# Layer 0 of a graph network: wider search chunks for the neighbour lists, biases on TensorE, row copies on ScalarE

## The chip, the core and the metric

The kernel runs on one core of one Trainium2 chip. The metric is the device time of one execution in microseconds; a difference is read from the medians of runs on the same chip. The engines are written as in the profile: PE (TensorE), PEld (its weight loads), DVE (VectorE), ACT (ScalarE), POOL (GpSimd), SP (SyncE, which here only issues transfers). L417 is line 417 of the kernel before.

## What is computed

A graph of n = 3327 nodes with 256 features each passes through four attention layers. The adjacency is a 0/1 matrix, symmetric, with ones on the diagonal and about 32 other neighbours a row. Layer 0 is the one that the change touches:

```python
g_src = nodes @ W_src_w.T + W_src_b
g_tgt = nodes @ W_tgt_w.T + W_tgt_b
g = leaky_relu(g_src[:, None, :] + g_tgt[None, :, :], 0.2)
score = where(adj != 0, einsum('ijc,c->ij', g, a_w), -inf)
x = layernorm(x + softmax(score, axis=1) @ g_tgt)
```

Layers 1 to 3 are attention layers whose scores split into a row and a column part; they are computed densely, on PE with DVE, and none of their code changes.

## The kernel before

**Layer 0 by lists.** Nodes are cut in 26 tiles of 128 rows and these in three sets of 5, 9 and 12 tiles (`SETS`). For each row the kernel finds the column numbers of its neighbours, and then fetches, for each of the up to 56 places of a list, one row of a table in HBM for each of 128 nodes (`gather`, L544, an indirect transfer that POOL issues). Within a set the rows are ranked by their number of neighbours, so that each later tile has fewer places (`LEVELS`).

**Projections** (`targets`, `sources`, L347 to L379). For each tile two products on PE (`project`, L342, contraction in two halves of 128) give the target row (256 features and one more column, the target's own part of the score) or the source row. DVE adds the target bias, L358, and takes the source with its bias and a turned sign, L374. ScalarE copies the one extra column, L359, and issues the writes of the row to the table `table_d` and to `own_d`, which holds for each node its source, its input x and its target row. The x part of `own_d` is copied from HBM to HBM by POOL's queue at the start, for all three sets (L327). The columns that PE needs are loaded by SP (L337, four buffers).

**The search** (`neighbours(s)`, L391 to L496). A tile's adjacency rows come in two halves of 1664 columns, loaded by SP (L122, called at L411; two buffers). L417 turns a half into 16-bit numbers: 0 where there is no edge, n minus the column where there is one; it sums them too. The diagonal is taken out (L426, L430). Then MAX8 (L436), an instruction that gives the eight largest of a row, is run on chunks of 64 columns, 52 a tile. The first three of each chunk go to a list `few` (L441), the best eight of the rest are added (L445): 164 numbers. From these, seven rounds of MAX8 and MATCH_REPLACE8 (L448, L450) draw 56. The sum of all numbers minus the sum of the 56 is stored in `lost` (L458): if it isn't zero for any row, the program repeats everything densely at its end (L1609). The numbers become column indices (L460), the count becomes a sort key, which a product on PE spreads over partitions (L481), and L490 with L494 make the ranks. POOL writes the lists to HBM in ranked order (`write_list`, L503) and reads them back (`read_lists`, L511).

**Scores and sums.** For each eight places (a part): `score` on DVE (L563, L569), and at the end of a tile `combine`: exponentials and scaling on ScalarE (L639, L650), adding up on PE (L653). `lay_out` on ScalarE (L559, L560) prepares a tile. `put_back` writes the sums (L689).

**Order of the work.** In this stage the order on PE, DVE, ACT and POOL is that of the program text. At first `neighbours(0)` runs in turn with the 26 `targets`, one of its 33 steps after each (L802). Then the lists of set 0 are written and read, and a loop over 126 parts (L862) issues at each part: a share of the steps of the next set's search (`owed`), work that is due at that part, the gathers of the part four ahead, and the scores. The lists of set 1 are written from part 17 on, those of set 2 from part 59. Eleven buffers hold gathered parts. SP isn't in this list: a planner of the compiler chooses the order on SP's queue, by readiness and place in the text; the load of the weight of layer 1 (L749), for example, belongs to a late part.[...] The dense layers follow when the sums are written.

Of the kernel before, what the change touches and what calls it, by code (L numbers as in the profile page):

```python
# [8 lines left out]
F32 = mybir.dt.float32  # L9
# [5 lines left out]
ALU = mybir.AluOpType  # L15
AX = mybir.AxisListType
# [3 lines left out]
P = 128  # L20
# [5 lines left out]


KMAX = 56
CHUNK = 64
FIRST = 3  # L30


SETS = (5, 9, 12)
# [6 lines left out]
FAR = 1e6  # L40

ROW = 260
# [4 lines left out]
def gat_stack(  # L47
# [29 lines left out]
    nc = tc.nc  # L77
    n, dim = x.shape
# [20 lines left out]

    h = [nodes.tile([P, dim], F32, name=f"h{it}") for it in range(nt)]  # L100
    at_d = dram.tile([nt * P, n], BF16, name="at_d")
    table_d = dram.tile([nt * P, ROW], F32, name="table_d")

    EARLY = sum(SETS[:-1])
    w1 = const.tile([P, kc, dim + 2], F32, name="w1")
# [10 lines left out]
    def copy_rows(engine, dst, src):  # L116

        rows = dst.shape[0]
        whole = rows // 16 * 16
        for lo, hi in ((0, whole), (whole, rows)):  # L120
            if lo < hi:
                engine.dma_start(dst[lo:hi], src[lo:hi])  # L122
# [139 lines left out]

    def sparse0(lost):
        GROUP, TURNS, LEAD = 8, 11, 4
        starts = [sum(SETS[:s]) for s in range(len(SETS))]
        with ExitStack() as s0:
# [11 lines left out]
                )  # L280
            )

            w_tgt = const0.tile([P, kc, dim + 1], F32, name="w_tgt0")
            nc.sync.dma_start(w_tgt[:, :, :dim], w_tgt_t.rearrange("(c p) f -> p c f", p=P))
            a_row = load_row(const0, a_w, "a_row")
            bt_row = load_row(const0, b_tgt, "bt_row")
            w_src = const0.tile([P, kc, dim], F32, name="w_src0")
            nc.scalar.dma_start(w_src, w_src_t.rearrange("(c p) f -> p c f", p=P))
            bs_row = load_row(const0, b_src, "bs_row")
            for c in range(kc):  # L290
                t = io0.tile([P, dim], F32, tag="minus", name="dots0")
                nc.vector.tensor_mul(t, w_tgt[:, c, :dim], a_row)
# [9 lines left out]
            for lo, hi in halves:  # L302
                hi = -(-hi // P) * P
                rev_i = io0.tile([P, nt * P // 2], I32, tag="adj_i", name="rev_i")
                nc.gpsimd.iota(
                    rev_i[:, : hi - lo], pattern=[[-1, hi - lo]], base=n - lo,
                    channel_multiplier=0,
                )
                nc.vector.tensor_copy(rev[:, lo:hi], rev_i[:, : hi - lo])
# [14 lines left out]
            for s, size in enumerate(SETS):  # L324
                lo, hi = starts[s] * P, min(n, (starts[s] + size) * P)
                own_d.append(dram.tile([size * P, OWN], F32, name=f"own{s}_d"))
                copy_rows(nc.gpsimd, own_d[s][: hi - lo, dim : 2 * dim], x[lo:hi, :])  # L327

            def own_rows(it):
                s = max(s for s in range(len(SETS)) if starts[s] <= it)  # L330
# [6 lines left out]
                nc.sync.dma_start(xt[:, :, :pn], x_t_p[:, :, it * P : it * P + pn])  # L337
                return xt, pn

            def project(p, xt, pn, weight):  # L340
                for k in range(kc):
                    nc.tensor.matmul(  # L342
                        p[:pn, : weight.shape[2]], xt[:, k, :pn], weight[:, k, :],
                        start=(k == 0), stop=(k == kc - 1),
                    )

            def targets(it):  # L347

                xt, pn = columns_of(it)
                row = io0.tile([P, ROW], F32, tag="row", name="row", bufs=3)  # L350
                nc.vector.memset(row[:, dim:], 0.0)
                if pn < P:
                    nc.vector.memset(row[:, :dim], 0.0)
                    nc.vector.memset(row[:, dim : dim + 1], -FAR)
                pt = ps0.tile([P, BANK], F32, tag="acc", name="pt")
                project(pt, xt, pn, w_tgt)
                yield
                nc.vector.tensor_add(row[:pn, :dim], pt[:pn, :dim], bt_row[:pn])  # L358
                nc.scalar.copy(row[:pn, dim : dim + 1], pt[:pn, dim : dim + 1])  # L359
                nc.scalar.dma_start(table_d[it * P : (it + 1) * P, :], row)  # L360
                nc.scalar.dma_start(own_rows(it)[:, 2 * dim :], row)
                yield

            def sources(it):

                xt, pn = columns_of(it)
                pss = ps0.tile([P, BANK], F32, tag="ps", name="pss", bufs=1)
                project(pss, xt, pn, w_src)
                yield
                minus = io0.tile([P, dim], F32, tag="minus", name="minus")  # L370
                if pn < P:
                    nc.vector.memset(minus, 0.0)
                    nc.scalar.dma_start(own_rows(it)[pn:, dim : 2 * dim], minus[pn:])
                nc.vector.scalar_tensor_tensor(  # L374
                    minus[:pn], pss[:pn, :dim], -1.0, bs_row[:pn],
                    op0=ALU.mult, op1=ALU.subtract,
                )
                nc.scalar.dma_start(own_rows(it)[:, :dim], minus)
                yield  # L379

# [6 lines left out]
            ]  # L387

            len_c = nt * P // CHUNK

            def neighbours(s):  # L391

# [7 lines left out]
                for t in range(size):  # L400
# [7 lines left out]
                    for b, (lo, hi) in enumerate(halves):  # L408
                        w, padded = hi - lo, -(-(hi - lo) // P) * P
                        adj_i = io0.tile([P, nt * P // 2], I32, tag="adj_i", name="adj_i")  # L410
                        copy_rows(nc.sync, adj_i[:pn, :w], adj[it * P : it * P + pn, lo:hi])  # L411
                        v = io0.tile([P, wider], U16, tag="num", name="num")
                        if pn < P:
                            nc.vector.memset(v, 0.0)
                        elif w < padded:
                            nc.vector.memset(v[:, w:padded], 0.0)
                        nc.vector.scalar_tensor_tensor(  # L417
                            v[:pn, :w], adj_i[:pn, :w], 0.0, rev[:pn, lo:hi],
                            op0=ALU.not_equal, op1=ALU.mult, accum_out=sums[:pn, b : b + 1],
                        )  # L420
                        if lo <= it * P < hi:

                            at0 = it * P - lo
                            own_v = v[:, at0 : at0 + P]
                            junk = io0.tile([P, P], F32, tag="junk", name="junk")
                            nc.vector.scalar_tensor_tensor(  # L426
                                junk, own_v, -1.0, ident, op0=ALU.mult, op1=ALU.mult,
                                accum_out=sums[:, 2:3],
                            )
                            nc.vector.tensor_mul(own_v, own_v, off_diag)  # L430
                        chunks = padded // CHUNK
                        for c in range(chunks):
                            if c == chunks // 2:
                                next(of_rows if b else before, None)
                                yield
                            nc.vector.max(  # L436
                                cand[:, lo // CHUNK + c, :], v[:, c * CHUNK : (c + 1) * CHUNK]
                            )
                        yield
                    few = io0.tile([P, FIRST * len_c + 8], F32, tag="few", name="few")  # L440
                    nc.vector.tensor_copy(  # L441
                        few[:, : FIRST * len_c].rearrange("p (c f) -> p c f", f=FIRST),
                        cand[:, :, :FIRST],
                    )
                    nc.vector.max(few[:, FIRST * len_c :], cand[:, :, FIRST:])  # L445
                    found = io0.tile([P, KMAX], F32, tag="found", name="found")
                    for r in range(0, KMAX, 8):
                        nc.vector.max(found[:, r : r + 8], few)  # L448
# [9 lines left out]
                    nc.vector.tensor_reduce(lost[:, it : it + 1], sums, axis=AX.X, op=ALU.add)  # L458
                    payload = io0.tile([P, KMAX + 2], U32, tag=f"pay{t}", name="payload", bufs=1)
                    nc.vector.tensor_scalar(  # L460
                        payload[:, :KMAX], found, -1.0, float(n), op0=ALU.mult, op1=ALU.add
                    )
                    nc.vector.tensor_copy(payload[:, KMAX : KMAX + 1], own_i[:, it : it + 1])
                    nc.vector.tensor_scalar_mul(
# [115 lines left out]
            def score(q):  # L580
# [6 lines left out]
                if k0 == 0:  # L587
                    sc = entry["sc"] = io0.tile([P, KMAX + 1], F32, tag="sc", name="sc", bufs=3)
                    if kt < KMAX:
                        at = nt + starts[s] + t  # L590
                        nc.vector.tensor_scalar(
                            lost[:, at : at + 1], entry["lst"][:, kt : kt + 1], float(n), None,
                            op0=ALU.is_lt,
                        )

                    y_own = io0.tile([P, 1, dim], F32, tag="y_own", name="y_own", bufs=1)
                    largest(y_own, own[:, None, 2 * dim : 3 * dim], minus_src, 1)
                    pen = io0.tile([P, 1], F32, tag="pen", name="pen")
                    nc.vector.tensor_scalar(
                        pen, entry["lst"][:, KMAX + 1 : KMAX + 2], 0.0, -FAR,  # L600
                        op0=ALU.is_equal, op1=ALU.mult,
                    )
# [174 lines left out]
            def project_next(it):  # L777
# [12 lines left out]
                for b, block in enumerate(blocks):  # L790
                    if it == block[-1]:
# [6 lines left out]
                        nc.scalar.copy(row[:t], m[:t])  # L798
                        nc.sync.dma_start(rate1_d[b][:, :], row[:t])


            first = neighbours(0)  # L802
            for it in range(nt):
# [40 lines left out]
            for it in range(SETS[0]):  # L844
                write_list(0, it)
            read_lists(0)


            ahead, owed, steps = [], {}, 0
# [821 lines left out]
```

The softmax here doesn't subtract the row's maximum and nothing guards it: scores larger than these inputs give would overflow.

## Time and profile before

| | us |
|---|---|
| median of 3 runs (3183.69 to 3191.36) | 3183.84 |
| the profiled execution | 3182.83 |
| its span, first to last instruction | 3181.0 |
| DVE busy | 2316.7 (73%) |
| PE busy | 2170.4 (68%) |
| POOL busy | 1042.3 (33%) |
| ACT busy | 734.7 (23%) |

The span is divided in three: up to about 168 us the startup (projections, search of set 0, first lists); up to about 1541 us gathers, scores and the search of sets 1 and 2; then the dense layers. POOL is busy almost only in the second.[...] A wait is written "engine tile line <- what ended it: us in total, times, longest". In a group the figures after the count are busy us, mean ns of one, and the idle time before them with what ended it.

### The profile page before, as it was taken

To read this page: it belongs to the slowest core of one execution; us is meant where nothing else is said; L and a number is where in the kernel's file an instruction comes from. 1 tells how busy PE (TensorE), PEld (TensorE's weight loads), DVE (VectorE), ACT (ScalarE), POOL (GpSimd) and SP (SyncE) were. 2 spreads that over 40 slices of the span, in tenths; PEclk is the share of its full clock that TensorE was granted. 3 is DMA by queue.
4 is the path that set the end of the run, shared out by engine and by line. 5 is a ranking of instruction groups with operands and counts; after the bars stand their busy time and mean duration, and the time that the engine had idled before them with its cause. 6 is when DMAs were issued, how large, how long until landed. Compare 5 with 4: busy or idle time off the path is not lost.

```text
span 3181.0 us, 44618 instructions
## 1 busy us (share of the span) xinstructions
PE 2170.4 (68%) x15572; PEld 1239.5 (39%) x15572; DVE 2316.7 (73%) x6592; ACT 734.7 (23%) x2068; POOL 1042.3 (33%) x1056
## 2 busy tenths in 40 slices
PE   4204324335352445443689999999999999999996
PEld 2102112112121222221468888885444445444332
DVE  6879999999976655555425552107888898899997
ACT  0003222324331434433234431120111110110110
POOL 0077747677767777777100000000000000000000
PEclk6556666667676677666799999999999999999998
DMA  7556536655434544444657663332212212212211
GB/s 208 156 138 175 154 99 164 172 152 163 123 83 111 136 109 120 117 118 114 190 145 216 200 189 91 109 104 82 65 47 70 67 49 68 67 48 57 57 47 46
DMA packets 177752, 367.93 MB, mean 116 GB/s; under 512 B 34340, under 2 KB 123236, under 8 KB 176494
## 3 DMA queue, kind: packets, MB, share of 16 engines
q1 hardware_dynamic: 95798, 171.81, 19.3%
q0 software_dynamic: 51424, 157.02, 18.9%
q10 hardware_dynamic: 30296, 36.15, 3.2%
q8 instruction: 125, 2.05, 0.3%
q14 instruction: 109, 0.89, 0.1%
HBM read 322.84 MB, written 45.43 MB: 116 GB/s over the span
## 4 chain that ended last, share of the span: by engine, by line
PE 45%; DVE 4%; DMA 1%; issue 0%; ACT 0%; POOL 0%; ACTq 0%; SPq 0%; DVEq 0%; POOLq 0%
PE acc L1326 17%; PE acc L1279 15%; PE acc L1334 8%; DVE e L1195 3%; PE misc L1125 3%; DMA at_i<-in_adj_t_dram 1%; DMA at<-at_d 1%; PE misc L1222 0%; PE misc L1408 0%; PE misc L1369 0%; DVE h L246 0%; DVE stats L1486 0%; DVE h L1484 0%; DVE h L1299 0%; DVE both L1481 0%
## 5 line engine op out<-in xcount | busy, mean ns | idle before, releaser
L544 POOL DMA_INDIRECT g<-table_d,lst x923 | 914.5, 991 | 296.4 <-issue 270.4
L1195 DVE SCALAR_TENSOR_TENSOR e<-rate,feat,at 128x896 f32<-128x896 f32 (+4 forms) x832 | 843.9, 1079 | 80.6 <-PE acc L1334 70.0
L653 PE MATMUL acc<-g,ident 128*128 128x512 f32 (+1 forms) x934 | 460.1, 651 | 414.3 <-ACT g L650 405.2
L1326 PE MATMUL acc<-e,feat 128*32 128x384 f32 (+2 forms) x6656 | 689.0, 516 | 4.8 <-DVE e L1195 2.1
L653 PEld LDWEIGHTS acc<-g,ident 128*128 128x128 f32 x934 | 195.7, 214 | 651.8 <-ACT g L650 426.5
L563 DVE TENSOR_TENSOR y<-g,both 128x1024 f32<-128x1024 f32 (+2 forms) x240 | 275.7, 1173 | 203.6 <-DMA g<-table_d,lst 194.6
L1326 PEld LDWEIGHTS acc<-e,feat 128*32 128x32 f32 x6656 | 259.2, 110 | 343.2 <-issue 233.8
L1334 PE MATMUL acc<-e,feat 128*32 128x384 f32 (+3 forms) x3328 | 375.6, 513 | 0.0
L650 ACT ACTIVATE g<-g,w 128x256 f32<-128x256 f32 x923 | 370.6, 493 | 0.0
L569 DVE SCALAR_TENSOR_TENSOR y<-y,both 128x256 f32<-128x256 f32 x923 | 324.6, 416 | 0.0
L1279 PE MATMUL acc<-feat,e 128*128 128x257 f32 (+2 forms) x1352 | 306.6, 383 | 23.6 <-DMA at_i<-in_adj_t_dram 14.4
L1279 PEld LDWEIGHTS acc<-feat,e 128*128 128x128 f32 (+2 forms) x1352 | 255.4, 191 | 63.7 <-issue 15.4
L240 POOL TENSOR_TENSOR rstds<-rstds,minus_half 128x7 f32<-128x7 f32 (+1 forms) x12 | 19.8, 1650 | 752.8 <-DVE rstds L239 752.8
L1279 PE MATMUL acc<-feat,at 128*128 128x257 bf16 (+2 forms) x2028 | 236.4, 273 | 7.0 <-DMA at<-at_d 6.7
L481 PE MATMUL key_rows<-key_diag,ones 128*128 128x128 f32 x52 | 17.7, 439 | 311.7 <-DVE key_diag L480 257.7
L1279 PEld LDWEIGHTS <-at 128*128 128x128 bf16 (+2 forms) x2028 | 197.7, 99 | 40.3 <-DMA at<-at_d 4.8
L1334 PEld LDWEIGHTS acc<-e,feat 128*32 128x32 f32 (+1 forms) x3328 | 139.3, 110 | 155.3 <-issue 131.8
L1195 DVE SCALAR_TENSOR_TENSOR e<-rate,feat,at_i 128x896 f32<-128x896 f32 (+2 forms) x104 | 111.1, 1079 | 94.9 <-ACT feat L1133 54.6
L436 DVE MAX8 cand<-num 128x8 f32<-128x64 uint16 x1352 | 179.0, 209 | 1.0
L1175 POOL DMA_DIRECT2D rate3b_d<-rate_rows x4 | 2.1, 520 | 467.2 <-ACT rate_rows L1174 467.2
L481 PEld LDWEIGHTS key_rows<-key_diag,ones 128*128 128x128 f32 x52 | 12.2, 278 | 324.9 <-DVE key_diag L480 214.3
L559 ACT COPY both<-own_of 128x256 f32<-128x256 f32 x26 | 9.7, 375 | 500.5 <-DMA own_of<-own_d,lst 367.4
(174 smaller groups left out, 1766.0 us busy)
## 6 DMA issues: line engine op xcount, KB each, us to landing
at<-at_d SPq DMA_DIRECT2D x150, 224.0 KB, 2.5
at_i<-in_adj_t_dram SPq DMA_DIRECT2D x50, 448.0 KB, 4.1
adj_i<-in_adj_dram SPq DMA_DIRECT2D x25, 832.0 KB, 4.6
adj_i<-in_adj_dram SPq DMA_DIRECT2D x25, 831.5 KB, 4.9
g<-table_d,lst POOLq DMA_INDIRECT x923, 2.8
at<-at_d SPq DMA_DIRECT2D x75, 192.0 KB, 2.4
at<-at_d SPq DMA_DIRECT2D x75, 191.8 KB, 2.4
at_d<-at ACTq DMA_DIRECT2D x50, 224.0 KB, 4.2
```

Of the source, the lines that this page charges most:

```text
L436: nc.vector.max(cand[:, lo // CHUNK + c, :], v[:, c * CHUNK : (c + 1) * CHUNK])
L481: nc.tensor.matmul(key_rows[:, t * P : (t + 1) * P], ones, key_diag, start=True, stop=True)
L544: nc.gpsimd.indirect_dma_start(out=g[:, k - k0, :], out_offset=None, in_=table_d[:, :], in_offset=bass.IndirectOffsetOnAxis(ap=entry["lst" ...
L563: nc.vector.tensor_tensor(y, rows, minus_src[:, None, :].to_broadcast([P, m, dim]), op=ALU.max)
L569: nc.vector.scalar_tensor_tensor(y, y, 1.0, a, op0=ALU.mult, op1=ALU.mult, accum_out=sc)
L650: nc.scalar.activation(rows, rows, AF.Copy, scale=w[:, k : k + 1])
L653: nc.tensor.matmul(dst, ident, rows, start=start, stop=stop)
L1125: nc.tensor.matmul(pacc[:pn, : dim + self.extra], ht[:, k, :pn], self.weight[:, k, :], start=(k == 0), stop=(k == kc - 1),)
L1195: nc.vector.scalar_tensor_tensor(e[:pn, : c1 - c0], self.rate[b][:pn, h_of, : c1 - c0], q, at[:pn, : c1 - c0], op0=ALU.max, op1=ALU.mult,)
L1279: nc.tensor.matmul(accs[s][:pn, : dim + 1], a[:pj, s * P : s * P + pn], f[:pj, : dim + 1], start=(j == 0 and part == 0), stop=(j == nt - 1 ...
L1326: nc.tensor.matmul(accs[x][p][q : q + 32, : hi - lo], f[:pj, at0 : at0 + 32], es[at0 // hd][:pj, lo:hi], start=(j == 0), stop=(j == nt - 1),)
L1334: nc.tensor.matmul(accs[x][pairs][h_of * 32 : (h_of + 1) * 32, : hi - lo], f[:pj, dim + h_of : dim + h_of + 1].to_broadcast([pj, 32]), es[ ...
```

## The change

`CHUNK` becomes 104, and a chunk consists of two runs of 52 columns that lie 832 apart within a half, so a tile has 32 chunks. Numbers become 4096 plus the column, so that no two of them add up to one. A ninth extra place of `few` takes what the listed numbers lack to the full sum, capped at the largest number. An empty place points to row 0 of the table, which has a score of -1e6; the table moves down by one row. Both biases enter as a third product on PE with one contraction row; a row of 260 columns leaves PSUM by one ScalarE copy, the source by one ScalarE multiplication. The x parts of `own_d` for sets 1 and 2 are issued by SP, in the text after the first lists are read.

```diff
-CHUNK = 64
+CHUNK = 104
+BASE = 4096
...
-    table_d = dram.tile([nt * P, ROW], F32, name="table_d")
+    table_d = dram.tile([n + 1, ROW], F32, name="table_d")
...
-            w_tgt = const0.tile([P, kc, dim + 1], F32, name="w_tgt0")
+            w_tgt = const0.tile([P, kc, ROW], F32, name="w_tgt0")
+            nc.vector.memset(w_tgt[:, :, dim:], 0.0)
-            bt_row = load_row(const0, b_tgt, "bt_row")
+            bt_row = const0.tile([1, ROW], F32, name="bt_row")
+            nc.vector.memset(bt_row, 0.0)
+            nc.sync.dma_start(bt_row[:, :dim], b_tgt[None])
-            bs_row = load_row(const0, b_src, "bs_row")
+            bs_row = const0.tile([1, dim], F32, name="bs_row")
+            nc.sync.dma_start(bs_row, b_src[None])
...
-                copy_rows(nc.gpsimd, own_d[s][: hi - lo, dim : 2 * dim], x[lo:hi, :])
+                if s == 0:
+                    copy_rows(nc.gpsimd, own_d[s][: hi - lo, dim : 2 * dim], x[lo:hi, :])
...
-                        start=(k == 0), stop=(k == kc - 1),
+                        start=(k == 0), stop=(k == kc - 1 and bias is None),
                     )
+                if bias is not None:
+                    nc.tensor.matmul(
+                        p[:pn, : weight.shape[2]], ones[:1, :pn], bias, start=False, stop=True
+                    )
...
-                nc.vector.memset(row[:, dim:], 0.0)
-                project(pt, xt, pn, w_tgt)
+                project(pt, xt, pn, w_tgt, bt_row)
                 yield
-                nc.vector.tensor_add(row[:pn, :dim], pt[:pn, :dim], bt_row[:pn])
-                nc.scalar.copy(row[:pn, dim : dim + 1], pt[:pn, dim : dim + 1])
-                nc.scalar.dma_start(table_d[it * P : (it + 1) * P, :], row)
+                nc.scalar.copy(row[:pn], pt[:pn, :ROW])
+                nc.scalar.dma_start(table_d[1 + it * P : 1 + it * P + pn, :], row[:pn])
...
-                project(pss, xt, pn, w_src)
+                project(pss, xt, pn, w_src, bs_row)
-                nc.vector.scalar_tensor_tensor(
-                    minus[:pn], pss[:pn, :dim], -1.0, bs_row[:pn],
-                    op0=ALU.mult, op1=ALU.subtract,
-                )
+                nc.scalar.mul(minus[:pn], pss[:pn, :dim], -1.0)
...
+                        spread_v = v[:, :padded].rearrange(
+                            "p (x c i) -> p c x i", x=2, i=CHUNK // 2
+                        )
                             nc.vector.max(
-                                cand[:, lo // CHUNK + c, :], v[:, c * CHUNK : (c + 1) * CHUNK]
+                                cand[:, lo // CHUNK + c, :], spread_v[:, c, :, :]
                             )
-                    few = io0.tile([P, FIRST * len_c + 8], F32, tag="few", name="few")
+                    few = io0.tile([P, FIRST * len_c + 9], F32, tag="few", name="few")
...
+                    nc.vector.tensor_reduce(
+                        sums[:, 3:4], few[:, : FIRST * len_c + 8], axis=AX.X, op=ALU.add, negate=True
+                    )
+                    lack = few[:, FIRST * len_c + 8 :]
+                    nc.vector.tensor_reduce(lack, sums, axis=AX.X, op=ALU.add)
+                    nc.vector.tensor_scalar_min(lack, lack, float(BASE + n - 1))
...
-                        payload[:, :KMAX], found, -1.0, float(n), op0=ALU.mult, op1=ALU.add
+                        payload[:, :KMAX], found, 1.0 - BASE, 0.0, op0=ALU.add, op1=ALU.max
...
+            none = io0.tile([1, ROW], F32, tag="row", name="none", bufs=3)
+            nc.vector.memset(none, 0.0)
+            nc.vector.memset(none[:, dim : dim + 1], -FAR)
+            nc.scalar.dma_start(table_d[0:1, :], none)
             first = neighbours(0)
...
             read_lists(0)
+            for s in range(1, len(SETS)):
+                lo, hi = starts[s] * P, min(n, (starts[s] + SETS[s]) * P)
+                copy_rows(nc.sync, own_d[s][: hi - lo, dim : 2 * dim], x[lo:hi, :])
```

## The prediction, made before the changed kernel was built

> **What bounds the kernel now.** I read the busy table by slices, then the waits, then the timeline of GpSimd (POOL) gap by gap, then the groups by shape of VectorE (DVE). First the busy times of chosen stretches (us busy and instruction counts; the last columns are TensorE clock, DMA share and GB/s):
>
> ```profile
> 120.00:160.00 40.00, 3.92 (x10) 2.28 (x10) 32.43 (x167) 0.16 (x1) 5.90 (x4) 0.54 0.38 116
> 400.00:480.00 80.00, 22.42 (x47) 10.42 (x48) 78.08 (x322) 21.29 (x56) 38.53 (x37) 0.61 0.34 102
> 640.00:720.00 80.00, 25.16 (x57) 12.31 (x57) 78.06 (x348) 20.57 (x54) 62.41 (x60) 0.63 0.51 150
> 1200.00:1280.00 80.00, 42.38 (x96) 19.32 (x96) 43.79 (x159) 30.94 (x87) 60.51 (x65) 0.71 0.44 115
> ```
>
> DVE (fourth number pair) is full until about 890 us and half idle after; POOL starts only at 143 us, has a hole at 400 to 480, and later issues 65 operations per 80 us, one gather each 1.25 us. The waits say who held POOL:
>
> ```profile
> POOL lists_d L503 <- DVE ranks_i L494: 135.7, 1, 135.7
> POOL lists_d L503 <- DVE lost L591: 24.9, 1, 24.9
> DVE num L417 <- DMA adj_i<-in_adj_dram: 16.3, 1, 16.3
> ```
>
> and, in POOL's timeline:
>
> ```profile
> 905.80 0.98 POOL L503 DMA_INDIRECT lists_d<-payload,ranks_i  x1 [10.24 <-DVE inv L676]
> ```
>
> Each of the three waits ends at the lists of one set (`neighbours(s)` done). So DVE sets the time from 27 us (first adjacency half arrives) to 143, and again up to 433, where the second lists are written. From 433 to 906 POOL and DVE run side by side: POOL loses 10.2 us at the third lists and 5.5 us in one gap at 613.8. After 906 POOL's gathers alone set the time to 1520; the layers behind start when the last sum is written.
>
> **The price of the search.** DVE up to 160 us, by shape:
>
> ```profile
> L436 DVE MAX8 cand<-num 128x8 f32<-128x64 uint16 x312 | 41.4, 210 | 0.2
> L448 DVE MAX8 found<-few 128x8 f32<-128x164 f32 x35 | 11.6, 332 | 1.2
> L358 DVE TENSOR_TENSOR row<-pt,bt_row 128x256 f32<-128x256 f32 x25 | 10.5, 419 | 11.4 <-PE pt L342 11.4
> L450 DVE MATCH_REPLACE8 few<-found,few 128x164 f32<-128x164 f32 x30 | 9.4, 313 | 0.0
> L374 DVE SCALAR_TENSOR_TENSOR minus<-pss,bs_row 128x256 f32<-128x256 f32 x5 | 2.0, 408 | 0.0
> L445 DVE MAX8 few<-cand 128x8 f32<-128x260 f32 x5 | 2.1, 426 | 0.0
> L455 DVE TENSOR_REDUCE sums<-found 128x1 f32<-128x56 f32 x5 | 1.0, 203 | 0.0
> ```
>
> Mean durations overlap a little; what counts is the distance of starts. 26 MAX8 of 64 columns take 3.30 us in the timeline (145.34 to 148.64), so 0.127 us each. L445 against L448: (426-332)/(260-164) = 0.98 ns a column.
>
> Per tile of 128 rows, on DVE:
> - Chunks: 52 x 0.127 = 6.60 becomes 32 x (0.127 + 40 x 0.00098) = 5.31: -1.29. That two runs of 52 cost no more than one run is taken from L445, whose input is runs of five columns and which still lies on the 0.98 ns line.
> - The list shrinks from 164 to 105: 59 x 0.00098 = 0.058 us in each of 7 MAX8 and 6 MATCH_REPLACE8: -0.75.
> - L441 and L445 read 60 and 100 columns less: -0.15.
> - Added: a sum over 104 (L455's 0.203 + 48 x 0.00098 = 0.25), a sum over four and a minimum of one column (0.15 each as L458, L464): +0.55 without overlap, +0.40 with it; I take 0.55.
> - L374 leaves: -0.33 by the distance of starts (54.02 to 54.35).
> Sum: 2.0 us less per tile (1.6 if the longer MAX8 cost 0.18, 2.2 with overlap).
>
> Per target tile L358 with its memset leaves: 0.34 us (37.43 to 37.77).
>
> **Startup (27.2 to 142.9 us).** 5 tiles x 2.0 = 10.0; 25 targets x 0.34 = 8.4; and the 11.4 us that DVE waited in L358 for TensorE have no successor, since DVE no longer reads the projections. Together 29.8. What could be late next:
> - TensorE. No product with one contraction row is in the trace; the nearest row is L342 itself, 12 records in 5.00 us, two records a product, so 0.83 us per bias product (nothing if its one row were free, 1.0 at a lower clock). Six records per target are 2.5 us. A DVE tile, 19.9 us now (49.90 to 69.77, five targets among it), becomes 16.2, and TensorE has six targets, one source and one key product in it: 15 + 2.5 + 0.8 = 18.3. It falls behind 2 us a tile, some 6 in all, and catches up in the last 7 of 33 steps, which hold no target. Cover gone at a lag of about 19 us.
> - ScalarE: L359 grows from 0.16 to about 0.38 (L559, 256 columns: 374 ns), sources add 0.38, the two DMA issues stay 0.8: 1.2 us per target, under 2.5. It is 23% busy; free. Its new waits are for TensorE's last product; behind them on its queue stand the row writes, later L559 and the exponentials. Today the same places wait for DVE (L559 behind L374: 133 us in all), so the wait is exchanged for an earlier one.
> - DMA. Shares of the first windows (0.86, 0.60 and 0.65 of 40 us, 0.38 of the last 23) sum to 93 us of full work; in 113 us that is 82%. Loads land later than the 5.3 us of now; an adjacency half has about 10 us of slack. I take off 3 us (bounds 0 and 15).
> So 27 us.
>
> **The moved copies.** own_d of sets 1 and 2 (2,687 KB) go from POOL's queue at 4.5 us to SP's. The text puts them behind the first lists, but SP's order is the planner's: it sends L749, belonging to a far later step, at 4.73 us, because nothing holds it. The copies are as free, so I expect them there, ahead of the first adjacency halves.
>
> ```profile
> 12.69 0.88 SPq L122 DMA_DIRECT2D adj_i<-in_adj_dram  x2
> ```
>
> and the transfers issued in the first 30 us (last number: us to landing):
>
> ```profile
> own_d<-in_x_dram POOLq DMA_DIRECT2D x1, 1520.0 KB, 18.9
> own_d<-in_x_dram POOLq DMA_DIRECT2D x1, 1152.0 KB, 13.0
> adj_i<-in_adj_dram SPq DMA_DIRECT2D x1, 831.5 KB, 16.1
> ```
>
> The two queues share today: both sides took 13 to 19 us together. The Trainium skill ("DMA: Bandwidth & Descriptors", "Queues, rings and completion order") says engines alternate between queue rows, but take descriptors of one row in ring order. By it the move harms: halves that alternated with the copies now stand behind all of them. Worked out at the 249 GB/s of these 30 us: about 5.7 MB lie up to the end of the first half (weights and rows 0.9, columns 0.5, copies 3.4, the half 0.85), 23 us from the 2 us at which the first moved: 25, if small packets go no slower; 33 if the copies run at half that. The row, same bytes before the same half, gives 27.2. I take 27.2, nothing gained or lost (bounds: +10 gain if the copies go out late and the half lands 4.5 us after 12.7; -6). Three issues of 0.45 us on SP cost nothing there, it is idle from 5.2 to 10.5. POOL is rid of some 2.3 us of issuing in a time in which it waits anyway. The new memsets (two column blocks, the bias row, row 0) are 0.1 to 0.3 us each and lie under the 16.3 us wait for the first half; the biases arrive as 1 KB instead of 128 KB each, 0.25 MB less.
>
> **First lists to second (143 to 433 us).** DVE bound. Of nine tiles about 0.7 is searched before POOL's first gathers land (DVE idles 17.5 us at L563 then), so 8.3 x 2.0 = 16.7. The wait of 24.9 is not used up by it: 8.2 would stay, and POOL itself would come earlier by what its gaps at 293, 364 and 405 (3.0, 3.9, 3.0) shrink, so 8 to 18.
>
> **To the third lists (433 to 906 us).** 12 x 2.0 = 24 us of DVE, but POOL then binds: what it gets is its own gaps, 10.2 + 5.5 = 15.7. What stays is this:
>
> ```profile
> 683.87 2.37 POOL L544 DMA_INDIRECT g<-table_d,lst  x1 [0.30 <-issue]
> ```
>
> beside DVE's timeline:
>
> ```profile
> 683.53 1.89 DVE L417 SCALAR_TENSOR_TENSOR num<-adj_i,rev 128x1664 uint16<-128x1664 int32 x1
> ```
>
> A gather that meets L417 takes 1.5 to 2.6 us instead of 0.95. The change keeps L417.
>
> After 906: nothing. Gathers are as many, the empty places read row 0 instead of row n, and POOL binds. The 1.8 us outside the span stay.
>
> **Sum.** 27 + 16.7 + 15.7 = 59.4 from the profiled execution's 3182.8: 3123.4. The median of the runs is 1.0 above that execution, so 3124.
>
> **Rivals.**
> - The copies do go late, or the first half lands early: 10 us more, and the DMA allowance comes back: 3111. For it: the text's order. Against: L749. 20%.
> - The gains stop halfway: longer MAX8 in two runs, adjacency loads late under an 82% busy DMA, POOL gaps that are not DVE's. Startup 15, second stretch 10, third 8: 33, so 3151. For it: startup DMA. Against: the waits name DVE. 25%.
> - Slower: adjacency loads L122 stand on SP's queue behind column loads L337, which wait for TensorE to free their buffers, which waits at the key product for DVE. Were that ring closed, each of tiles 2 to 4 and the first of set 1 would add TensorE's 18.3 and a landing of 5.3: 4 x 23.6 = 94, less 59 gained: 3219. It turns the sign from 15 us per tile. Against: loads go out 13 to 20 us ahead of their use today, and DVE waited for one only once. 3%.
> - It doesn't do what it says: rows that lose two neighbours would call the dense repeat. Counted over the adjacency that the setup makes, rows have at most 52 neighbours and 32 chunks in two runs lose none. 1%, thousands of us.
> Forecast itself 51%.
>
> **Range and chances.** 3105 to 3152: from somewhat beyond the early-landing case to the halfway case. Faster by over 0.3% (9.6 us, about what a measurement of this kernel can tell) 0.95, within 0.02, slower 0.03.
>
> **What would show it.** L436 at about 0.17 us apart, x832; L358 gone and no DVE wait on the projections; ranks of set 0 at 116 (143 before); the wait at the second lists 8 to 18 us, at the third gone; gather spacing after it 1.25 as before. Wrong if L417 waits for adj_i more than once in the startup, if the first half lands before 20 or after 33 us, or if the stage after the third lists changes length.

## The result, and the profile after

The changed kernel takes 3142.37 us (median of 4 runs, 3138.89 to 3146.09), the kernel before beside it 3187.35 us (3183.69 to 3191.36): a ratio of 0.9859, 95% interval 0.9839 to 0.9879. The time is inside the range on record, but 45 us were gained where 59 were forecast. With the kernel before at 3187 instead of the 3184 that the forecast started from, the time is 18 us above the number given. The profiled execution took 3138.89 us (span 3137.0), against 3182.83 (3181.0).

Lines move: L417 is L425 now, L436 is L448, L448 is L467, the projection L342 is L351 with the bias product at L356, the gather L544 is L563, L503 is L522. Three times at which POOL begins to write lists divide the gain:

| POOL begins to write | before, us | after, us | earlier by | added since the row above | forecast for that step |
|---|---|---|---|---|---|
| first lists | 143.26 | 129.67 | 13.6 | 13.6 | 27 |
| second lists | 433.23 | 405.64 | 27.6 | 14.0 | 16.7 |
| third lists | 905.80 | 859.22 | 46.6 | 19.0 | 15.7 |
| the last sums | 1540.84 | 1495.32 | 45.5 | -1.1 | 0 |

The span ends 44.0 earlier. So the middle is about right, its halves are off in opposite directions, and half of the startup's gain is missing. The waits of the changed kernel up to 140 us, and after that two of POOL's list writes from its timeline:

```profile
POOL lists_d L522 <- DVE ranks_i L513: 124.3, 1, 124.3
DVE num L425 <- DMA adj_i<-in_adj_dram: 17.5, 2, 16.0
DVE row L365 <- DMA own_d<-row: 13.3, 1, 13.3
```

```profile
405.64 0.98 POOL L522 DMA_INDIRECT lists_d<-payload,ranks_i  x1 [20.26 <-DVE lost L610]
```

```profile
859.22 0.98 POOL L522 DMA_INDIRECT lists_d<-payload,ranks_i  x1 [0.80 <-DVE inv L695]
```

The wait of 10.24 at the third lists is gone, the one of 24.85 at the second is still 20.26. Two things in the waits are new. The second line has two waits for adjacency, of 16.0 and 1.5 us, where the kernel before had one; the forecast named a second one as a sign of being wrong. And DVE, which had no more to do with the projections, stands 13.3 us at one (third line). L365 is `memset(row, 0)` of the last target, which has fewer than 128 rows. There are three row buffers, so it waits for the row of target 22 to be written out, and that row waits for TensorE. The stretches show TensorE's side (us; PE, PEld, DVE, ACT, POOL busy with their counts; PE clock, DMA share, GB/s):

```profile
40.00:80.00 40.00, 37.45 (x74) 20.43 (x74) 37.96 (x177) 4.14 (x11) 0.00 (x0) 1.00 0.59 173
80.00:120.00 40.00, 40.00 (x79) 21.34 (x78) 23.98 (x111) 4.89 (x13) 0.00 (x0) 1.00 0.63 193
...
640.00:720.00 80.00, 31.63 (x78) 15.71 (x76) 77.90 (x325) 18.23 (x47) 61.86 (x61) 0.68 0.57 168
1200.00:1280.00 80.00, 37.28 (x91) 16.98 (x89) 43.08 (x156) 29.21 (x80) 60.51 (x65) 0.76 0.46 113
```

From 80 to 120 us PE is busy all of the time, and it is DVE that idles (24 of 40). From 640 on the picture is that of before: DVE full, POOL 62 of 80 us; after the third lists (859 us) POOL's gathers alone. PE's and PEld's timelines in the bound stretch:

```profile
101.19 2.10 PE L351 MATMUL pt<-w_tgt,xt 128*128 128x260 f32 x4
103.22 1.23 PE L356 MATMUL pt<-bt_row,ones 1*128 1x260 f32 x2
104.38 2.10 PE L351 MATMUL pt<-w_tgt,xt 128*128 128x260 f32 x4
```

```profile
101.19 1.37 PEld L351 LDWEIGHTS pt<-w_tgt,xt 128*128 128x128 f32 x4 [0.65 <-issue]
103.22 0.50 PEld L356 LDWEIGHTS pt<-bt_row,ones 1*128 1x128 f32 x2 [0.66 <-issue]
```

From one target to the next, 101.19 to 104.38, are 3.19 us: 2.03 for the four full records and 1.16 for the two with one contraction row. The forecast allowed 2.5. PEld shows something that the kernel before doesn't have in its startup: 0.66 us of idle time, without a wait that the profile names, before each change between full and one-row weights. From one key product to the next, 42.55, 65.29, 88.03 and 110.77, TensorE takes 22.74 us for a tile's six targets and one source; DVE's tile takes 16.6 (L425 starts at 42.41 and 59.00).

The search, by shape, up to 132 us, and 16 chunks of it in DVE's timeline:

```profile
L448 DVE MAX8 cand<-num 128x8 f32<-128x104 uint16 x162 | 28.3, 251 | 0.2
L467 DVE MAX8 found<-few 128x8 f32<-128x105 f32 x35 | 9.5, 270 | 1.2
L469 DVE MATCH_REPLACE8 few<-found,few 128x105 f32<-128x105 f32 x30 | 7.6, 254 | 0.0
L459 DVE TENSOR_REDUCE sums<-few 128x1 f32<-128x104 f32 x5 | 1.3, 261 | 0.2
```

```profile
78.14 2.78 DVE L448 MAX8 cand<-num 128x8 f32<-128x104 uint16 x16
80.87 0.06 DVE L424 MEMSET num<- 128x1 uint16 x1
```

Sixteen in 2.73 us: 0.171 us apart, about as forecast (5.31 / 32 = 0.166). The first line's 251 ns is the mean of one, overlap included; what counts is the distance.

### The profile page after: what moved, and what is told of

Its sections match the earlier page's. It is cut to its first block, busy times and chain, and to the rows that moved or that the text cites. A ratio compares the mean times of both kernels' runs of the same rounds, so it can differ in the third digit from the quotient of the medians.

```text
span 3137.0 us, 44325 instructions
## 1 busy us (share of the span) xinstructions
PE 2235.7 (71%) x15676; PEld 1263.2 (40%) x15676; DVE 2259.3 (72%) x6075; ACT 749.6 (24%) x2094; POOL 1039.5 (33%) x1053
## 4 chain that ended last, share of the span: by engine, by line
PE 45%; DVE 4%; DMA 2%; issue 1%; ACT 0%; POOL 0%; ACTq 0%; SPq 0%; DVEq 0%; POOLq 0%
PE acc L1353 17%; PE acc L1306 15%; PE acc L1361 8%; DVE e L1222 3%; PE misc L1152 3%; DMA at<-at_d 1%; DMA at_i<-in_adj_t_dram 1%; PE misc L1249 0%; PE misc L1435 0%; PE misc L1396 0%; DMA h<-sums_d 0%; DVE stats L1513 0%; DVE h L248 0%; DVE h L1511 0%; DVE h L1326 0%
## 5 line engine op out<-in xcount | busy, mean ns | idle before, releaser
L563 POOL DMA_INDIRECT g<-table_d,lst x923 | 916.9, 993 | 282.1 <-issue 265.5
L448 DVE MAX8 cand<-num 128x8 f32<-128x104 uint16 x832 | 145.6, 251 | 1.0
L1239 ACT CAST at<-at_i 128x896 bf16<-128x896 int32 (+2 forms) x104 | 92.0, 885 | 97.0 <-DMA at_i<-in_adj_t_dram 74.3
```

Of the source, the lines that this page charges most:

```text
L448: nc.vector.max(cand[:, lo // CHUNK + c, :], spread_v[:, c, :, :])
L563: nc.gpsimd.indirect_dma_start(out=g[:, k - k0, :], out_offset=None, in_=table_d[:, :], in_offset=bass.IndirectOffsetOnAxis(ap=entry["lst" ...
L1239: nc.scalar.copy(at[:pn, :w], at_i[:pn, :w])
```

## The experiments

**The chips.** The ten runs below were made on three chips on which the kernel before takes about 13% longer (medians 3590.1, 3620.3 and 3591.1 us): from about 200 us on, DVE is in stretches given an instruction only each 1.40 us. The cause isn't known. The startup isn't touched (the control's first lists come at 129.2 and 129.0 us, 129.7 in the profile above). So the startup is read from these profiles directly, and whole times only as ratios to the kernel before on the same chip. These ratios mostly came out nearer to 1 than the expectations have them; the theories are judged by the startup.

**The theory, P:** the bias products set TensorE's pace in the startup, and DVE gets its early lists only as fast as projections come. The rivals put something else in its place: the transfers, which the hoisted copies delay; the memset that binds DVE to the row buffers; what is fixed in the order of PE's program. The letters in the expectations are theirs.

### The search alone

The changed search, with biases and the turned sign on DVE as before and the copies on POOL at the start.

```diff
-project(pt, xt, pn, w_tgt, bt_row)
+project(pt, xt, pn, w_tgt)
...
-nc.scalar.copy(row[:pn], pt[:pn, :ROW])
+nc.vector.tensor_add(row[:pn, :dim], pt[:pn, :dim], bt_row[:pn])
+nc.scalar.copy(row[:pn, dim:], pt[:pn, dim:ROW])
```

> The changed search alone: both biases and the turned sign back on DVE (L358 and L374 as before), the copies of all sets back on POOL's queue. Theory A (the prediction's sum: each part gives what it takes from DVE): 1.3 us a tile without the 0.33 of L374, by the changed trace's own spacing (MAX8 0.171 us apart); 5 tiles in the startup, 8.3 to the second lists, 12 to the third: 6 + 11 + 15 = 32 us, so about 3151 for the profiled execution, ratio 0.990; ranks of set 0 at about 137 us. Theory B (the two runs of 52 or the longer chain of small operations give most of it back): ratio 0.997 or more.

Measured: 3559.53, ratio 0.9912 (0.9889 to 0.9935); first lists at 134.79 us. That is 8.5 us before those of the kernel before. Of these, 1.1 are the first half, read at 26.09 instead of 27.23; the rest is about 1.5 us for each of five tiles (from tile to tile 21.40 us instead of 22.86). The old wait is back at its old size:

```profile
DVE row L366 <- PE pt L348: 11.5, 5, 2.7
```

(The memset of each row's last columns, 0.06 us beside another instruction, isn't back in this kernel.) So of the startup's 13.6 us this kernel has 8.5, and all that was moved off DVE brings only 5.1, where the forecast had 8.4 + 11.4 for it. Over the whole kernel this half of the change (0.9912) can't be told from the full one (0.9917 and 0.9945 in the control runs, on other chips).

### Bias products over 128 rows

The same arithmetic, with 127 rows of zeros added to each bias row (`bs_row` likewise), so that every product has 128 contraction rows.

```diff
-bt_row = const0.tile([1, ROW], F32, name="bt_row")
+bt_row = const0.tile([P, ROW], F32, name="bt_row")
...
-p[:pn, : weight.shape[2]], ones[:1, :pn], bias, start=False, stop=True
+p[:pn, : weight.shape[2]], ones[:, :pn], bias, start=False, stop=True
```

> As the changed kernel, but the bias product contracts over all 128 rows: the bias lies in row 0 of a 128-row tile of zeros, and the ones are the whole 128 x 128 tile. Same sums. Theory P (TensorE sets the startup, because a product with one contraction row can't overlap its weight load with its neighbours): a projection falls from 3.19 us to 2.6 or less, TensorE is no longer full at 80 to 120 us, DVE's wait of 13.3 us at the memset of the last target row goes, ranks of set 0 at 116 us instead of 129.7, about 13 us less in all: ratio to the kernel before 0.982. Rival K (a product costs the same whatever its number of contraction rows): 3.19 us and 129.7 unchanged, ratio 0.986. Rival T (transfers set the startup): unchanged too.

Measured: 3555.82, ratio 0.9893 (0.9857 to 0.9928); first lists at 113.91 us, 15.8 earlier than the change as it stands (P had 116). PE's timeline, then the stretches:

```profile
92.15 1.94 PE L352 MATMUL pt<-w_tgt,xt 128*128 128x260 f32 x4
93.89 1.07 PE L357 MATMUL pt<-bt_row,ones 128*128 128x260 f32 x2
94.75 1.94 PE L352 MATMUL pt<-w_tgt,xt 128*127 128x260 f32 x4
96.48 0.82 PE L357 MATMUL pt<-bt_row,ones 128*127 128x260 f32 x2
97.14 1.03 PE L352 MATMUL pss<-w_src,xt 128*128 128x256 f32 x4
98.00 0.59 PE L357 MATMUL pss<-bs_row,ones 128*128 128x256 f32 x2
```

```profile
40.00:80.00 40.00, 28.66 (x101) 23.41 (x102) 38.04 (x179) 6.04 (x16) 0.00 (x0) 0.76 0.77 235
80.00:120.00 40.00, 17.61 (x61) 13.36 (x59) 37.27 (x161) 3.40 (x9) 2.43 (x1) 0.71 0.62 190
```

A target takes 2.60 us where PE has just stood still (92.15 to 94.75), and after some microseconds the same six records run at nearly twice that rate: the source at 97.14 has its four full records in 0.86 us, 2.00 with one-row products between them. PE has 101 records from 40 to 80 us instead of 74, in 28.7 instead of 37.5 us; DVE is full in both stretches, and its wait at the memset is gone. A product with more rows is the cheaper one here. P is right; what is fixed in PE's order, and the transfers, would have left the first lists at 129.7. That a weight load can't overlap its neighbours, which the expectation gives as the reason, isn't shown by any run; the profile has idle time and no cause for it.

The two paces go with the granted clock, but the clock column must be read with care. Stretches of this run, and then of the change (the clock is the third column from the end):

```profile
7.00:11.00 4.00, 4.00 (x10) 3.13 (x11) 2.18 (x5) 0.13 (x1) 0.00 (x0) 1.00 1.05 280
80.00:84.00 4.00, 4.00 (x21) 3.45 (x19) 3.96 (x17) 0.75 (x2) 0.00 (x0) 1.00 0.98 314
92.00:96.00 4.00, 4.00 (x11) 3.18 (x11) 3.93 (x18) 0.38 (x1) 0.00 (x0) 0.50 0.60 168
```

```profile
0.00:7.00 7.00, 0.00 (x0) 0.00 (x0) 2.06 (x10) 0.00 (x0) 4.74 (x12) 1.00 0.70 173
100.00:104.00 4.00, 4.00 (x9) 2.17 (x8) 0.00 (x0) 0.00 (x0) 0.00 (x0) 1.00 0.76 214
```

At 1.00 there are 21 records in 4 us, at 0.50 there are 11. From 7 to 11 us there are 10 beside a 1.00: the slow pace. The trace's first record of the clock, a stretch at full clock, begins at about 12 us, and before it the column prints 1.00. In the change the first record, at full clock too, begins at about 266 us, so the 1.00 of its whole startup, the 7 us before any product included, is no reading. The pace there is the one that goes with 0.50 elsewhere.

### The copies back on POOL's queue

```diff
-if s == 0:
+if True:
...
-copy_rows(nc.sync, own_d[s][: hi - lo, dim : 2 * dim], x[lo:hi, :])
```

(The first condition surrounds the copy at the start; the second line is the later one, taken out.)

> As the changed kernel, but the copies of sets 1 and 2 are back on POOL's queue at the start. Theory P: TensorE sets the startup, and it idled 3.5 us for a row write that stood behind the copies and 3.6 us for columns, so at most 7 us less, ranks of set 0 at 123 to 130 us. Rival T (standing behind the copies in SP's own row costs the startup): first adjacency half earlier than 25.7 us, ranks before 122. If the order on the row made no difference, the first half stays at 25 to 28 us and the total within 3 us of the changed kernel.

Measured: 3562.72, ratio 0.9919 (0.9899 to 0.994); the first half is read at 25.92 us, first lists come at 129.30. With the copies on SP's queue, ahead of the half, it is read at 25.69. In SP's timeline of the change:

```profile
4.67 9.23 SPq L124 DMA_DIRECT2D own_d<-in_x_dram  x3
...
16.58 1.57 SPq L124 DMA_DIRECT2D adj_i<-in_adj_dram  x2
```

The copies did go out first, as the forecast had it, and held SP for 9.2 us (1.4 were reckoned); the half went out at 16.58 instead of 12.69 and still landed 1.5 us earlier. The ring order of the Trainium skill ("DMA: Bandwidth & Descriptors", "Queues, rings and completion order"), which was weighed against the move, makes no difference that can be seen: 25.69 behind the copies on one queue, 25.92 beside them on another, where the half was issued at 12.92.

### The copies late

Where the text has them, but issued by ScalarE, whose order is the text's.

```diff
-copy_rows(nc.sync, own_d[s][: hi - lo, dim : 2 * dim], x[lo:hi, :])
+copy_rows(nc.scalar, own_d[s][: hi - lo, dim : 2 * dim], x[lo:hi, :])
```

> As the changed kernel, but the copies of sets 1 and 2 are issued by ScalarE, whose order is that of the text, so that they do go out after the first lists are read. The first adjacency half should land near 18 us instead of 25.7 in any case. Theory P: DVE then starts 7 us earlier, but TensorE's 105 us of projections set the end; it starts without its 3.5 and 3.6 us waits, so ranks of set 0 at 122 to 126, 4 to 7 us less in all. Rival T (transfers set the startup): ranks at 117 or earlier, 12 us less.

Measured: 3560.66, ratio 0.9917 (0.9898 to 0.9936); the first half is read at 18.08, first lists at 121.45, just below P's 122 to 126 and above the other theory's 117.

```profile
DVE row L365 <- DMA own_d<-row: 12.6, 1, 12.6
DVE num L425 <- DMA adj_i<-in_adj_dram: 10.1, 2, 8.5
```

```profile
40.00:80.00 40.00, 40.00 (x78) 21.00 (x76) 36.63 (x168) 4.47 (x12) 0.00 (x0) 1.00 0.64 191
```

The copies do cost the start 7.6 us, on either queue, and without them the lists come 8.2 earlier. But the wait at the memset stays at 12.6, and PE is still full, with 22.74 us a tile as before: the whole startup has shifted, TensorE's pace in it hasn't changed. The rival that transfers hold the projections back is out; had they, more than 8 us would have come back.

### The change again, and both cures

The control is the change unaltered; the other kernel has the full-row products and the late copies.

> The changed kernel unaltered, beside the kernel before on one chip, as the control of the runs sent with it. Every theory expects 0.986 of the kernel before if the chip behaves as the first one, and ranks of set 0 at 129.7 us.

> As the changed kernel, with both cures together: the bias product over 128 rows (row 0 the bias, the others zero), and the copies of sets 1 and 2 issued by ScalarE behind the first lists. Theory P (TensorE set the startup, and with it gone DVE does, from the landing of the first half on): the first half lands at 18.3 us and ranks come 88 us after it (113.9 - 25.2 in the run with full rows), at 107 us, 22 us before the changed kernel's 129.7; all later stretches as in the changed kernel, so 22 us less in all, ratio 0.979. Rival T (transfers are the floor once TensorE is free): the copies' 2.7 MB now collide with the gathers instead and their gain of 7 is given back: ratio 0.982.

Measured: control 3584.82, ratio 0.9917 (0.9886 to 0.9948), first lists at 129.15; both cures 3572.38, ratio 0.9872 (0.9833 to 0.9911), first lists at 105.68. The gains add up to a microsecond (129.15 - 15.8 - 8.2 = 105.2). Whole times differ by 12 us, with intervals that overlap; the last experiment has a clearer comparison.

### Bias products over 64 rows

Two readings of P were left: the change of the number of rows between neighbouring products costs, or a nearly empty array doesn't keep the faster rate. With 64 rows the array is half full, and the number changes as before.

```diff
-p[:pn, : weight.shape[2]], ones[:1, :pn], bias, start=False, stop=True
+p[:pn, : weight.shape[2]], ones[:64, :pn], bias, start=False, stop=True
```

> As the changed kernel, but the bias product contracts over 64 rows (row 0 the bias, 63 of zeros). Theory P1 (what costs is the change of row count between neighbouring products: the next weights can't be loaded until the array is empty): projections stay at 3.19 us, ranks at 129. Theory P2 (what costs is a nearly empty array, which keeps the clock at half): with 64 rows the clock rises at least at times, projections fall to 2.6 or below, ranks at 114 to 120.

Measured (one run, 3588.33): first lists at 129.75. PE and PEld:

```profile
66.16 1.94 PE L352 MATMUL pt<-w_tgt,xt 128*128 128x260 f32 x4
68.03 1.23 PE L357 MATMUL pt<-bt_row,ones 64*128 64x260 f32 x2
69.19 2.10 PE L352 MATMUL pt<-w_tgt,xt 128*128 128x260 f32 x4
```

```profile
68.03 0.50 PEld L357 LDWEIGHTS pt<-bt_row,ones 64*128 64x128 f32 x2 [0.66 <-issue]
69.19 1.37 PEld L352 LDWEIGHTS pt<-w_tgt,xt 128*128 128x128 f32 x4 [0.66 <-issue]
```

1.16 us and 0.66 us to the hundredth, as with one row. So it isn't the emptiness of a one-row product. With 64 rows the slower rate stays too. But a different number of rows isn't enough either: the kernel before has, in a later layer, products of 127 rows between products of 128. Its PEld timeline, one of 128 rows and one of 127 at the same place:

```profile
1952.07 0.25 PEld L1222 LDWEIGHTS misc<-ident,h 128*128 128x128 f32 x2
1957.84 0.25 PEld L1222 LDWEIGHTS misc<-ident,h 127*128 127x128 f32 x2
```

No idle time stands before the second, nor before the full rows behind it (these are bf16; f32 products of 127 rows beside 128, later in the same trace, at 2551.57, show none either). What costs are 1 and 64 rows beside 128; between 64 and 127 nothing was measured. That the array must be empty first, as the expectation has it, isn't shown.

### No memset on DVE

The missing rows of the last target are written from the table's constant row 0, which gets a place of its own, so DVE has no part in the row buffers.

```diff
-if pn < P:
-    nc.vector.memset(row, 0.0)
...
-nc.scalar.dma_start(own_rows(it)[:, 2 * dim :], row)
+nc.scalar.dma_start(own_rows(it)[:pn, 2 * dim :], row[:pn])
+if pn < P:
+    nc.scalar.dma_start(own_rows(it)[pn:, 2 * dim :], none)
```

> As the changed kernel, but the last target tile's row isn't cleared by DVE (its one row without a node gets the constant row of the table's row 0 instead), so that DVE doesn't wait for a free row buffer. Theory P (TensorE is late, and the memset only the place where DVE meets it): DVE runs on, the 13.3 us wait goes, and it waits at L509 for TensorE's last key product instead, which comes when the projections are through, near 122 us: ranks at 125 to 127, 3 to 5 us less. Rival M (the clearing's wait for a buffer is the cause by itself, TensorE is not late): ranks at 116, 13 us less.

Measured (one run, 3589.2): first lists at 125.85. The 13.3 us are gone from L365, but only 3.8 come back.

```profile
DVE junk L509 <- PE key_rows L500: 4.8, 1, 4.8
```

DVE waits 4.8 us for PE's key product at L509 instead, which stands behind the projections in PE's order, and once more for adjacency (23.6 in three waits, 17.5 in two). The memset is where TensorE's lateness showed, not its cause; for the most part another wait takes its place.

### All three cures

Full-row products, late copies and no memset. (The expectation calls it the same kernel as the one with two cures; it has the third as well.)

> The same kernel as the one with bias products over 128 rows and late copies, once more, to see what it is worth where the gather stages run as in the profiles shown. Theory P: ranks of set 0 at 106 us, 24 earlier than in the change as it stands; if the stages behind keep that lead, 24 us less than the change, about 3118 us where the kernel before takes 3187. Rival: part of the lead is given back at the second lists, as in the run before (rest 5 to 15 us), so 3127 to 3137.

> The change as it stands, as the control beside it: 0.986 of the kernel before, ranks of set 0 at 129.5 us.

Measured: 3552.56, ratio 0.9885 (0.9863 to 0.9906), against 3574.61, ratio 0.9945 (0.9925 to 0.9966) for the change as it stands: 22 us, and the intervals are apart. POOL begins to write the three lists at 105.6, 512.2 and 1131.6 us against 129.0, 533.1 and 1161.1, so the startup's 23.4 us are kept in the main (20.9 at the second lists, 29.4 at the third). It beats the change by these 22 us and the kernel before by 39. That the ratio for the change is 0.9859 above and 0.9917 and 0.9945 on these chips shows how far chips differ. What this version is worth where the kernel before takes 3187 us wasn't measured; 3142 - 22 = 3120 is an estimate.

## Why the prediction was right and where it was wrong

**Which engine sets the end, right.** DVE up to the second lists, DVE with POOL up to the third, POOL alone after. The last stretch, forecast at nothing, measured 1.1 us more.

**The failed step: TensorE's price.** "Six records per target are 2.5 us" took the bias product at the row's 0.83 and left its neighbours as they were. At this pace, six full-row records of 260 columns take 2.60 (92.15 to 94.75 in the run with full rows), so the pace was priced right. What was put at nothing is the change of rows: with one-row products between them, the four full records take 2.03 instead of 1.74 and the two bias records 1.16 instead of 0.86, together 3.19 a target. A tile is then 22.74 us of TensorE and not 18.3; DVE's tile is 16.6 where 16.2 was reckoned. TensorE falls behind 6.1 us a tile and not 2, about 18 in three tiles. "Cover gone at a lag of about 19 us" stood there as the condition, and it came true, by a path that wasn't named: the memset that kept DVE bound to the row buffers, where it waited 13.3 us. The bounds (0 and 1.0 for the product) were too narrow because they priced the new product alone. The upper one, "at a lower clock", had nothing to stand on: the 0.83 was read from 47.6 us on, where the clock column shows 0.50 up to 52. With 2.60 a target the lag would be some 2 us a tile, as forecast (an estimate). With the full-row products, where TensorE had time to spare, the startup came out at about the forecast: 29.3 us earlier (143.26 to 113.91), 2.4 of them from an earlier first half; 27 was forecast.

A weight of one row itself is no slower: 308 ns in the group of its loads, 326 for one of 128 rows. So the Trainium skill's statement ("TensorE: Matmul & The Clock Gate", "LDWEIGHTS (loading the stationary operand)") that a load's time comes from its columns and not its contraction rows agrees with the trace, and would have led to the same wrong 2.5: what costs is the 0.66 us of idle time before the loads, where loads between full rows have 0.10.

That TensorE also stayed at the slow pace was, for the forecast, no error, since it reckoned with no other. But at the faster one it wouldn't have been late: the change's own source at 289.04, six records of both kinds, takes 1.58 us.

```profile
289.04 1.03 PE L351 MATMUL pss<-w_src,xt 128*128 128x256 f32 x4
290.00 0.69 PE L356 MATMUL pss<-bs_row,ones 1*128 1x256 f32 x2
```

```profile
289.99 0.29 PEld L356 LDWEIGHTS pss<-bs_row,ones 1*128 1x128 f32 x2 [0.33 <-issue]
```

Seven such groups and a key product would be some 12 us a tile (an estimate from these lines), under DVE's 16.6. The Trainium skill ("TensorE: Matmul & The Clock Gate", "What's actually happening") has the clock at full after some 3.4 us of sustained activity. The run with full rows agrees: PE starts at 41.64, 58.24, 74.90 and 91.57, and the fast pace is there some 4 to 5 us later. In the change PE is busy without a break from 42.55 to 120.8 us and stays at the slow pace; the first rise, at about 266 us, comes some 4 us after PE starts on a long row of full-row products (262.58). So the profile's "busy" isn't what raises the clock here; what of the activity counts, no run shows.

**The search's 2.0 us per tile measured 1.6.** Chunks 6.60 to 32 x 0.171 = 5.46, so 1.14 of the 1.29. The rounds, from the first MAX8 to the start of the last, 4.75 to 4.02 in the timeline, 0.73 of the 0.75. The added sums cost 0.68 instead of 0.55 (36.23 to 36.91). L374 is taken at its 0.33 and L441 with L445 at their 0.15. All measured terms have the right sign, all are a little short. The search alone, without the 0.33, gave about 1.5 in the startup, where these terms make 1.3. The argument that two runs of 52 cost no more than one was circular (L445 was one of the two points through which the 0.98 ns line was drawn), and right all the same: 0.171 against 0.166.

**First to second lists, a size.** 8.3 tiles x 1.6 = 13.3; measured 14.0. The remaining wait of 20.3 lies just above the "8 to 18" given: POOL came 9.4 us earlier, within the 9.9 of the three gaps named, and DVE 2.7 less early than forecast (24.9 - 14.0 + 9.4 = 20.3).

**To the third lists, too cautious.** The forecast let POOL's two large gaps bound it at 15.7. It was 19.0, close to DVE's 12 x 1.6 = 19.2; the two come to the third lists almost together now (0.80 us of waiting), so that the lines don't say which of them bounds. The wait at the lists gave 9.4. POOL's waits, of before from 430 and of after from 400 us, both to 910, show that the largest hole, 5.5, closed too:

```profile
POOL g L544 <- issue: 92.9, 288, 5.5
...
POOL g L544 <- DMA g<-table_d,lst: 5.3, 12, 1.4
```

```profile
POOL g L563 <- issue: 96.5, 315, 0.8
...
POOL g L563 <- DMA g<-table_d,lst: 0.9, 3, 0.3
```

Most of the rest lay in small waits for landings, 5.3 against 0.9.

**The copies, right.** The place (first, since nothing holds them) and the landing (27.2 forecast, 25.69 measured). Their issue on SP was 9.2 us, not three times 0.45; the first half was issued 3.9 us later for it and still landed earlier. **ScalarE, right:** 375 ns for the row's copy and 0.38 us for the source, 0.38 forecast. TensorE waited for it once, 3.5 us up to 23.47, while ScalarE itself had stood 11.1 us at a wait that ended with the copies' transfer.

**The rivals.** The halfway case had startup 15, then 10 and 8, in all 33; measured are 13.6, 14.0 and 19.0. It had the startup right, for another reason (it named longer MAX8 and late loads). The whole gain, 45, lies between the two, in part by luck: the third stretch gave 3.3 us more than forecast and hid as much of the startup's miss. Late copies gave their 8 us in an experiment, but the change doesn't make them late. The slower case and the repeat didn't happen.

**Still open:** why 1 or 64 rows beside 128 expose idle time before the weight loads, and why TensorE keeps the slower pace while it lasts. The exposed time isn't a consequence of the slow pace: at the fast one it is still there, 0.33 us (lines above). That it is the cause of the slow pace fits all runs, but nothing separates it from the number of rows itself.

## What to carry to other kernels

Moving an addition to another engine is priced at that engine's pace in that stage, neighbours included: compare tile time with tile time, and if the new engine comes out within a few microseconds, the answer hangs on a price not yet measured. On TensorE, a product of few contraction rows between full ones can cost more than a full one, by itself and by the pace of the others: pad it with zeros to 128 rows and measure. A clock of 1.00 in the profile counts only from the trace's first clock record on; compare it with the time of known products. A wait that appears at some other instruction (here a memset) names the buffer, not the cause; taking the instruction away moved the wait.

## What the runs showed that wasn't expected

Between full products of 260 columns, a one-row or 64-row product costs 1.16 us instead of 0.86 and takes them from 1.74 to 2.03, and TensorE stays at the slower of its two paces; 128 rows, mostly zeros, end both, and the startup gets 15.8 us shorter. One row fewer, 127 beside 128, exposes nothing. Three copies from HBM to HBM held SP's queue 9.2 us at issue. On three chips the kernel before takes about 13% longer than in the runs shown first, with DVE in stretches receiving an instruction each 1.40 us.
